# Fewer sparse products in the first two periods, six at the head of the later ones, and shorter scalar chains

## The chip, the core and the metric

One core of one Trainium2 chip runs the whole kernel in one launch. The metric is the device time of that launch in microseconds (us). Engines are named as in the profile: PE (TensorE matmul), PEld (its weight loads, which overlap PE), DVE (VectorE), ACT (ScalarE), POOL (GpSimd) and SP (SyncE, which issues most DMAs). Each engine runs its own instructions in program order and waits on semaphores for the others.

## The reference

```python
# x (2708, 256), adj (2708, 2708): about 0.3% of it nonzero, and its diagonal
x = layernorm(x + relu(concat([x, adj @ x], 1) @ weight + bias))      # layer 0

def top_p_attention(X):                 # W1, W3: (64, 256), W2: (64, 64)
    q = X @ W1.T @ W2.T
    k = X @ W3.T
    probs = softmax(q @ k.T)            # (2708, 2708)
    idx = argsort(-probs)
    sp = take_along_axis(probs, idx)
    cs = cumsum(sp)
    keep = cs - sp < 0.9                # the largest ones, up to 0.9 of the mass
    A = probs * scatter(keep, idx)
    return A / A.sum(-1)

R = adj + eye(N)
R = R / R.sum(-1)
Z, Xf, Xa = 0, x, x                     # layer 1
for n in range(2):
    A = top_p_attention(Xa)
    Xf = R @ Xf
    Xa = A @ Xa
    Z = Z + Xf @ U1[n].T + Xa @ U2[n].T
out = layernorm(x + layernorm(x + Z))   # the inner one with gain and bias
```

So there are two rounds of a 2708 x 2708 attention, in each of which every row is cut at 0.9 of its mass, and two products with a sparse matrix R.

## The kernel before

Rows are cut into 22 blocks of 128 (the last, the edge, has 20). The first part of the run, up to about 742 us, does layer 0, the first attention and the projections. The change lies in the second attention, a loop over 24 periods, `for per in range(NB + 2)`, each of six groups, `for g in range(NG)`. Some 23 to 26 us make a period, and in period `per` four blocks are in work at once:

- Block `per + 2` gets its logits and exponentials. The logits come in three chunks (L535 on PE, chunk 0 already in the last group of the period before, chunks 1 and 2 at groups 1 and 3). There is one buffer in PSUM for them, so a chunk waits until ACT has read the one before (L885, and L889 for a second, flatter exponential of chunk 0). L882 on DVE takes a row shift from chunk 0.
- Block `per + 1` is tried at two levels, on ACT (`try_act`): at each a pass with Relu (L1027) and one with Sign (L1030) over 2708 columns, and then a chain of operations on [128x1] numbers (L1033 to L1043) that gives the next level. DVE prepares the first level in `begin_search` (L893 to L898) and takes the results up in `last_level` (L1064 to L1074).
- Blocks `per` and `per - 1` are on DVE: one pass that drops what lies above the level (L1084), candidates (L1091), their order (L1100, L1103), a threshold (L1119 to L1139), marks (L1144), and the mask (L1149).
- Block `per - 2` is multiplied: PE turns the masked rows, four 128x128 tiles a group (`turn`, L562), ACT copies them from PSUM (L564), and PE multiplies them with `ya` (`products`, L591), two groups later.

Between these stand the products of R. Row block `m` of R is eight units, seven of gathered rows and one of its own rows, each one matmul of 256 columns (L788, two rows in the profile) summed in PSUM. There are two sweeps over the 22 row blocks, `s = 0` with `yf_d` and `s = 1` with `v_d`, the result of the first. With each unit POOL may issue one indirect DMA (`y_rows`, L745) that gathers rows for the unit two row blocks ahead; the gathered rows have three slots (`yg[:, m % 3]`). At the start of a row block SP issues the loads of R's part two row blocks ahead (`adjp` has three buffers). At its end DVE scales the sum and adds a base (`r_out`, L817 for the first sweep, `arrive`, L833 for the second), one or two groups later through the list `later`. Sixteen of the 352 units come before the loop; the number in a period is `units[per]`, and they are spread evenly over the six groups:

```python
n = n_r * (g + 1) // NG - n_r * g // NG
```

In group 0 they stand ahead of the block's first transposes, in later groups behind the transposes of the group. Periods 2 to 9 end the first sweep, period 10 has none, and periods 11 to 21 have the second sweep at 16 a period.

In the second sweep finished rows are normalised as they come (`final_slot`): statistics on DVE (L1240) at groups 3 and 4, L1276 and L1277 on ACT at group 5, and at group 0 of the next period L1250 on ACT and two adds and products on POOL (L1265, L1266), behind the gathers that POOL has been given up to then. What POOL leaves is what L1240 reads at group 4.

The small numbers of a block lie in one tile, `self.all`; `b.l0`, `b.l1`, `b.l2` are levels, `b.u0`, `b.u1` what lies above them, `b.few` and `b.kept` are used by `last_level`.

Of the kernel before, what the change touches and what calls it, by code (L numbers as in the profile page):

```python
# [11 lines left out]
AF = mybir.ActivationFunctionType  # L12
ALU = mybir.AluOpType
# [4 lines left out]
TOP_P = 0.9  # L18
# [15 lines left out]
STEPS = ((0.97048, 13.37709, 72.87486), (1.01755, 9.09506, 145.60103))  # L34
FEW = 17.8171
# [4 lines left out]
ML = 16  # L40
CW, CC = 128, 7
EARLY = 12
AT = 96


# [17 lines left out]
def gnn_two_layer_kernel(ctx: ExitStack, tc: tile.TileContext, N, xT_d, x_d, adj_d, w0_d, b0_d,  # L63
# [30 lines left out]
    assert SEG * (NS - 1) + 8 <= N <= SEG * NS == SEG2 * NS2 and N >= SEG2 * (NS2 - 1) + 8  # L94
    assert SEG * NS - P == (NB - 1) * P - AT and AT + N - (NB - 1) * P <= P
    assert NB == 3 * KS + 1 and CW == P and CAP % 8 == 0 and N < NB * P
# [63 lines left out]
def fast_path(ctx, tc, c, flags, fint, xT_d, x_d, w0_d, b0_d, w1_d, w2_d, w3_d, u1_d, u2_d, g_d, b_d):  # L160
    nc = tc.nc
    N, D, DA, NB, DC, KH, CHS, rows = c.N, c.D, c.DA, c.NB, c.DC, c.KH, c.CHS, c.rows
# [17 lines left out]
    def ps_acc(t=None):  # L180
        acc = ps.tile([P, CH], FP, tag="acc", name="acc")
        if t == NB - 1:
            nc.vector.memset(acc[:, :D + 1], 0.0)
        return acc
# [11 lines left out]
    b0 = es[1][:, :D]  # L196
# [272 lines left out]
    lists = Lists(0, ML, flags[:, NF - 4:NF - 2], first_room)  # L469
    order = list(range(EARLY)) + [EDGE] + list(range(EARLY, EDGE))  # L470
    for m, prev, then in zip(order, [None] + order, order[1:] + [None]):
# [37 lines left out]
        if ML <= m < EDGE:  # L509
            i, n = m - ML, EDGE - ML  # L510
# [14 lines left out]
    def logits(s, t, i):  # L525


        p = rows(t)
        lg = ps_lg()
        cs = KPS[2 * i:2 * i + 2]  # L530
        skip = CH - (cs[0][1] - cs[0][0])
        for h, (a, b) in enumerate(cs):
            o = slice(DA * h, DA * h + DA)
            at = (skip, 0)[h]
            nc.tensor.matmul(lg[:p, h, at:at + b - a], lhsT=q[o, t * P:t * P + p], rhs=keys[s][o, i, :b - a],  # L535
                             start=True, stop=True)
        a, b = cs[0][0], cs[-1][1]
        return lg.rearrange("p h n -> p (h n)")[:p, skip:skip + b - a], a, b
# [7 lines left out]
    NG = (NB + 3) // 4  # L546
# [80 lines left out]
    def exps1(t):  # L627

        p = rows(t)
        e = es[t % 4]  # L630
        nmax, srt = st1[t]
        z = small.tile([P, 2], FP, tag="z1", name="z1", bufs=3)
        st1[t] = (srt, z)
        h = 11 * P

        def part(i):
            if i == 0:
                nc.scalar.activation(srt[:p], srt[:p], AF.Exp, bias=nmax[:p], scale=1.0)
            a, b = ((0, h), (h, N))[i]
            nc.scalar.activation(e[:p, a:b], e[:p, a:b], AF.Exp, bias=nmax[:p], scale=1.0,  # L640
                                 accum_out=z[:p, i:i + 1])
        return part
# [46 lines left out]
    def ya_pair():  # L689
# [15 lines left out]
        p = rows(t0 + 1)  # L705
        nc.scalar.copy(ya[AT:AT + p, t0 + 1, :], pz[:p, 1, :])

# [95 lines left out]
    def za_load(m):  # L803


        if loads.get(m):
            loads[m] = 2
            return None
        loads[m] = 1
        base = work.tile([P, D], FP, tag="in", name="base", bufs=3)  # L810
        nc.sync.dma_start(out=base[:rows(m)], in_=za_d[m * P:m * P + rows(m), :])
        return base
# [36 lines left out]
    def e2(t):  # L849
        return ring[t % 5]  # L850
# [30 lines left out]
    def shift(b, lg):  # L881
        nc.vector.tensor_reduce(b.nmax, lg[:, :P], AX.X, ALU.max, negate=True)  # L882
# [8 lines left out]
    def begin_search(b):  # L891

        nc.vector.tensor_reduce(b.z, b.all[:b.p, :NL], AX.X, ALU.add)  # L893
        yield
        nc.vector.reciprocal(b.rz, b.z)
        nc.vector.tensor_scalar(b.nz, b.z, -1.0, None, op0=ALU.mult)
        yield
        nc.vector.tensor_scalar(b.l0, b.roots, b.roots, b.rz, op0=ALU.mult, op1=ALU.mult)  # L898

    def run_all(steps):  # L900
        for _ in steps:
            pass
# [22 lines left out]
    part = exps1(0)  # L925
# [5 lines left out]
    part = exps1(1)  # L931
# [11 lines left out]
    for t in range(NB):  # L943
        acc = ps_acc(t)
        part = exps1(t + 2) if t + 2 < NB else None
        b = None
        if t >= NB - 3:
            b = blocks[t - (NB - 3)] = Block(t - (NB - 3))
        ra_next = finish1(t + 1) if t + 1 < NB else None
        if t == 0:  # L950
            nc.vector.memset(x1_edge, 0.0)
            nc.vector.tensor_copy(x1_edge[AT:AT + rows(EDGE)], x1[:rows(EDGE), EDGE, :])
        for g in range(NG):
# [39 lines left out]
    scale, turn_out, project = ends  # L993
# [22 lines left out]
    def fifth():  # L1016
        nonlocal scr
        tile2 = big.tile([P, 2 * NW], FP, tag="V", name="e4")
        ring.append(tile2[:, :NW])
        scr = tile2[:, NW:]  # L1020

    def try_act(b, k, part):


        e = e2(b.t)[:b.p, :N]
        if part == 0:
            nc.scalar.activation(scr[:b.p, :N], e, AF.Relu, bias=b.nz, scale=b.l[k], accum_out=b.relu)  # L1027
            return
        if part == 1:
            nc.scalar.activation(scr[:b.p, :N], e, AF.Sign, bias=b.nz, scale=b.l[k], accum_out=b.sign)  # L1030
            return
        if part == 2:
            nc.scalar.activation(b.n, b.sign, AF.Identity, bias=halfn[:b.p], scale=0.5)  # L1033
            return
        nc.scalar.activation(b.u[k], b.relu, AF.Identity, bias=b.n, scale=b.rz)
        next_level(b, k)

    def next_level(b, k):
        keep, slope, down = STEPS[k]
        nc.scalar.activation(b.kept, b.l[k], AF.Copy, scale=keep + TOP_P * slope, bias=-down)  # L1040
        nc.scalar.activation((b.l1, b.l2)[k], b.u[k], AF.Identity, bias=b.kept, scale=-slope)
        if k:
            nc.scalar.activation(b.few, b.l1, AF.Copy, scale=TOP_P, bias=-FEW)  # L1043

    def level(b, l):

# [266 lines left out]

    each = NB * (CC + 1)
    first = 2 * (CC + 1)
    units = {0: 12, 1: 20}
    rest = each - first - sum(units.values())
    units.update({p: rest * (p - 1) // 8 - rest * (p - 2) // 8 for p in range(2, 10)})
    units.update({p: each * (p - 10) // 11 - each * (p - 11) // 11 for p in range(11, 22)})
# [3 lines left out]
    b0, b1, b2 = (blocks[t] for t in range(3))  # L1323
# [3 lines left out]
    try_dve(b0, 1)  # L1327
    run_all(begin_search(b2))
    try_act(b0, 1, 0)
    next_level(b0, 1)  # L1330
    lg = logits(1, 3, 0)
    r_units(CC + 1)
    r_outs()
# [2 lines left out]
    for per in range(NB + 2):  # L1336
        if per == 1:
            fifth()
        if per == NB + 1:
            tail.append(True)  # L1340
        n_r = units.get(per, 0)
        b_act = blocks.get(per + 1)
        t_mul = per - 2 if per > 1 else None
        if t_mul is not None:
            accs[t_mul] = ps_acc(t_mul)
        b_exp = None
        if per and per + 2 < NB:
            b_exp = blocks[per + 2] = Block(per + 2)
        vector = vector_slots(blocks.get(per), blocks.get(per - 1), begin_search(b_exp) if b_exp else None)
        for g in range(NG):  # L1350
            n = n_r * (g + 1) // NG - n_r * g // NG
            now = later.pop(0)
            later.append([])
            if g == 0:
                if b_exp:
                    shift(b_exp, lg[0])
                r_units(n)
            if t_mul == EDGE:
                if g == 0:
                    products(0)  # L1360
                    products(0)
                    edge_product(ya, accs[EDGE], e2(EDGE))
            elif t_mul is not None:
                turn(t_mul, g, ya, accs[t_mul], e2(t_mul))
            if b_exp and g == 3:
                lg = logits(1, b_exp.t, 2)
            if g == NG - 1 and 3 < per + 3 < NB:
                lg = logits(1, per + 3, 0)
            if g:
                r_units(n)  # L1370
            if b_exp and g == 1:
                lg = logits(1, b_exp.t, 1)
            if t_mul is not None and t_mul != EDGE:
                products(2)
            if b_exp and g in (0, 1, 3):
                exps2(b_exp, (g + 1) // 2, *lg)
            if b_act:
                for k, part in {0: ((0, 0),), 1: ((0, 1), (0, 2), (0, 3)), 2: ((1, 0),), 3: ((1, 1), (1, 2), (1, 3))}.get(g, ()):
                    try_act(b_act, k, part)
            if per == 0:  # L1380
                ya_pair()
            next(vector)
            if per == 2 and g == 1:
                nc.gpsimd.memset(ring[4][:, N:], 0.0)
            if g == 0:
                final_slot(0)
                if t_mul:
                    t = t_mul - 1
                    base = za_load(t)
                    later[1].append(lambda t=t, base=base: arrive(t, base, accs.pop(t), ras.pop(t)[:rows(t)]))  # L1390
            for f in now:
                f()
            if g and (per < NB + 1 or g < NG - 1):
                final_slot(g)
# [4 lines left out]
    for f in later[0] + later[1]:  # L1399
# [10 lines left out]
                                   op0=ALU.mult, op1=ALU.is_lt)  # L1410
# [9 lines left out]
    n = len(new) + len(finals)  # L1420
# [384 lines left out]
```

## Time and profile before

| what | value |
|---|---|
| median of 6 runs | 1307.95 us (1298.33 to 1315.97) |
| the profiled execution | 1303.53 us, its span 1301.7 us |
| PE busy over the span | 1206.0 us, 93% |
| DVE busy | 975.7 us, 75% |
| ACT busy | 733.4 us, 56% |
| POOL busy | 643.9 us, 49% |
| mean granted clock of TensorE | 0.972 |
| products of R (L788) after 742 us, each half a unit | 387 to 393 ns by the profile's rows |

The profile is of one execution. Matmuls overlap: a row of L788 is recorded as some 0.39 us, but in a run of them one starts about 0.22 us after another, so a unit of two rows takes 0.43 us of PE when PE runs on. The granted clock is given with stretches of the trace; at 0.50 a row takes twice as long. "issue" in brackets behind an idle time says that the profile shows nothing the engine waited for; for logits (L535) it is then the one buffer. Busy time over the whole span hides that the loop's stages have different bounds, so the tables that follow go by stretches of time.

### The profile page before, as it was taken

Reading aid. Unit: us, or ns where it says so; the run is one execution under the profiler, and the core shown is the slowest. Engines: PE = TensorE matmul, PEld = TensorE weight load, DVE = VectorE, ACT = ScalarE, POOL = GpSimd, SP = SyncE. Lnnn points to the kernel's source line nnn. Section 1 sums busy time; section 2 is a strip of 40 time slices with the busy share of each in tenths; the row PEclk is TensorE's granted clock in tenths of the full one; section 3 lists DMA queues with packets and bytes.
Section 4 is the critical chain, followed back from the end, with each engine's and each line's share of the span. In section 5 each row is a group of like instructions: output and inputs, shape, how many; then the busy total and the mean of one; then the engine's idle time right before and its main releaser. Section 6 shows DMA issues by size and latency. Waiting matters only on the chain.

```text
span 1301.7 us, 18668 instructions
## 1 busy us (share of the span) xinstructions
PE 1206.0 (93%) x5772; PEld 910.5 (70%) x5772; DVE 975.7 (75%) x3254; ACT 733.4 (56%) x1299; POOL 643.9 (49%) x596
## 2 busy tenths in 40 slices
PE   7999999999799999999996997999998899999875
PEld 6888878853577777766774575777776677776754
DVE  2455554976999888877751377898999889988886
ACT  2010111045565566655562478798999789988822
POOL 1000000014735533677566377788826868888860
PEclk9999999999899999999998798999999999999988
DMA  7465535434222110223223355565524545555441
GB/s 194 148 205 170 170 124 166 150 107 127 61 91 74 53 60 10 78 92 106 86 70 109 106 162 176 164 185 169 163 71 148 173 141 160 163 186 151 146 116 39
DMA packets 104248, 164.92 MB, mean 127 GB/s; under 512 B 20162, under 2 KB 76870, under 8 KB 104138
## 3 DMA queue, kind: packets, MB, share of 16 engines
q1 hardware_dynamic: 77852, 107.57, 25.9%
q0 software_dynamic: 20544, 51.17, 14.5%
q10 hardware_dynamic: 5742, 4.89, 1.4%
q8 instruction: 48, 0.79, 0.3%
q14 instruction: 62, 0.51, 0.1%
HBM read 129.66 MB, written 33.90 MB: 126 GB/s over the span
## 4 chain that ended last, share of the span: by engine, by line
PE 71%; ACT 10%; DVE 6%; issue 5%; POOL 3%; DMA 2%; another core or an unknown queue 2%; SPq 0%; ACTq 0%; POOLq 0%; DVEq 0%
PE acc L591 25%; PE acc L274 13%; PE lg L535 9%; PE misc L788 8%; PE tr L562 7%; POOL yg L745 3%; PE acc L678 2%; ACT e L885 2%; ACT e L1030 2%; PE acc L699 2%; ACT wT L564 2%; PE misc L727 1%; PE misc L449 1%; DMA yg<-v_d,ix 1%
## 5 line engine op out<-in xcount | busy, mean ns | idle before, releaser
L564 ACT COPY wT<-tr 128x512 f32<-128x512 f32 (+2 forms) x258 | 136.3, 537 | 232.9 <-PE tr L562 154.7
L591 PE MATMUL acc<-x,wT 128*128 128x256 f32 x882 | 222.6, 393 | 19.1 <-ACT wT L564 15.6
L745 POOL DMA_INDIRECT yg<-v_d,ix x154 | 197.1, 1280 | 76.6 <-issue 36.6
L591 PE MATMUL acc<-ya,wT 128*128 128x256 f32 x924 | 227.8, 388 | 3.6 <-issue 3.5
L745 POOL DMA_INDIRECT yg<-yf_d,ix x154 | 193.5, 1257 | 75.1 <-issue 36.1
L591 PEld LDWEIGHTS acc<-x,wT 128*128 128x128 f32 x882 | 161.4, 193 | 81.6 <-issue 31.5
L591 PEld LDWEIGHTS acc<-ya,wT 128*128 128x128 f32 x924 | 174.3, 193 | 43.9 <-issue 21.8
L274 PE MATMUL acc<-y,adj_t 128*128 128x257 f32 x924 | 204.4, 379 | 0.0
L274 PEld LDWEIGHTS acc<-y,adj_t 128*128 128x128 f32 x924 | 173.7, 189 | 26.8 <-issue 1.9
L384 POOL DMA_INDIRECT adj_t<-in_adj,ix x154 | 163.9, 1064 | 51.2 <-issue 43.7
L562 PE MATMUL tr<-ident,e 128*128 128x128 f32 (+1 forms) x946 | 147.7, 275 | 17.7 <-DVE e L1149 12.5
L535 PE MATMUL lg<-k,q 64*128 64x512 f32 (+3 forms) x528 | 139.8, 605 | 24.8 <-ACT e L542 9.4
L788 PE MATMUL misc<-yg,adj_t 128*128 128x256 f32 (+1 forms) x602 | 159.5, 393 | 2.1 <-DMA yg<-v_d,ix 1.9
L562 PEld LDWEIGHTS tr<-ident,e 128*128 128x128 f32 (+1 forms) x946 | 119.5, 144 | 54.6 <-issue 24.3
L351 POOL DMA_DIRECT2D part_d<-e x1 | 0.6, 576 | 274.1 <-DVE e L350 274.1
L788 PEld LDWEIGHTS misc<-yg,adj_t 128*128 128x128 f32 (+1 forms) x602 | 105.9, 190 | 41.5 <-issue 21.7
L1027 ACT ACTIVATE e<-e,st 128x2708 f32<-128x2708 f32 (+1 forms) x43 | 113.6, 2641 | 0.0
L1030 ACT ACTIVATE e<-e,st 128x2708 f32<-128x2708 f32 (+1 forms) x42 | 110.9, 2641 | 0.0
L462 ACT COPY x1T<-tr 128x256 f32<-128x256 f32 (+1 forms) x22 | 8.0, 364 | 174.6 <-PE tr L461 174.6
L597 DVE MAX8 cand<-e 128x8 f32<-128x170 f32 (+1 forms) x352 | 86.6, 319 | 21.3 <-ACT e L542 15.1
L1091 DVE MAX8 cand<-w 128x8 f32<-128x170 f32 (+1 forms) x352 | 94.4, 323 | 0.1
L535 PEld LDWEIGHTS lg<-k,q 64*128 64x128 f32 (+1 forms) x528 | 40.0, 185 | 57.7 <-issue 31.7
(254 smaller groups left out, 1799.8 us busy)
## 6 DMA issues: line engine op xcount, KB each, us to landing
adj_t<-in_adj SPq DMA_DIRECT2D x42, 704.0 KB
adj_t<-adjc_d SPq DMA_DIRECT2D x44, 448.0 KB
adjc_d<-adj_t SPq DMA_DIRECT2D x22, 256.0 KB
base<-za_d SPq DMA_DIRECT2D x40, 128.0 KB
adjc_d<-adj_t SPq DMA_DIRECT2D x22, 192.0 KB
xt<-in_x ACTq DMA_DIRECT2D x21, 128.0 KB
x_d<-x SPq DMA_DIRECT2D x21, 128.0 KB
x1b_d<-xb SPq DMA_DIRECT2D x21, 128.0 KB
```

The costliest lines, as they stand in the source:

```text
L274: nc.tensor.matmul(acc[:p, :n], lhsT=halves[k // KH][:, k % KH, :p], rhs=y[:, k, :n], start=k == 0, stop=stop and k == NB - 1)
L384: nc.gpsimd.indirect_dma_start(out=a[:CW, i, :], out_offset=None, in_=adj_rows, in_offset=bass.IndirectOffsetOnAxis(ap=ix[:CW, m, i:i + 1] ...
L535: nc.tensor.matmul(lg[:p, h, at:at + b - a], lhsT=q[o, t * P:t * P + p], rhs=keys[s][o, i, :b - a], start=True, stop=True)
L562: nc.tensor.transpose(tr[:, k % 4, :p], columns(e[:p], k), ident[:p, :p])
L564: nc.scalar.copy(wT[:, :len(ks), :p], tr[:, :len(ks), :p])
L591: nc.tensor.matmul(acc[:p, :D], lhsT=wT[:, k % 4, :p], rhs=part_y(y, k), start=k == 0, stop=k == NB - 1)
L597: nc.vector.max(dst[:p, i * 8:(i + 1) * 8], src[:p, i * step:i * step + w])
L745: nc.gpsimd.indirect_dma_start(out=yg[:CW, m % 3, i, :], out_offset=None, in_=rows_d, in_offset=bass.IndirectOffsetOnAxis(ap=ix[:CW, m, i: ...
L788: nc.tensor.matmul(acc[:p, :D], lhsT=a[:kw, k, :p], rhs=y[:kw, k, :] if k < CC else own[:p], start=k == 0, stop=k == CC)
L1027: nc.scalar.activation(scr[:b.p, :N], e, AF.Relu, bias=b.nz, scale=b.l[k], accum_out=b.relu)
L1030: nc.scalar.activation(scr[:b.p, :N], e, AF.Sign, bias=b.nz, scale=b.l[k], accum_out=b.sign)
L1091: nc.vector.max(b.cand[:p, 8 * i:8 * i + 8], low[:p, SEG2 * i:SEG2 * (i + 1)])
```

## The change

- `units` is 8 and 12 in periods 0 and 1 instead of 12 and 20. What is left over, 140 instead of 128, is spread over periods 2 to 9: 17 or 18 instead of 16.
- From period 2 on, six of a period's units (`HEAD`) stand in group 0, ahead of the first transposes, and the rest is spread over groups 1 to 5. With 16 units the groups have 6, 2, 2, 2, 2, 2 instead of 2, 3, 3, 2, 3, 3. Each unit takes its gather, its loads and its `r_out` along.
- The small chain of the first level on ACT no longer passes through `b.u0`: `begin_search` prepares a scale and an offset on DVE (two more [128x1] operations a block), and the chain writes `b.l1` in its second operation. `b.kept` and `b.few`, which hang on `b.l1` alone, follow it there (`from_level`) instead of in the second level's chain. The first chain keeps four operations, the second has three instead of five.

```diff
--- before.py
+++ after.py
@@ -40,6 +40,7 @@
 ML = 16
 CW, CC = 128, 7
 EARLY = 12
+HEAD = 6
 AT = 96
 
 
@@ -895,7 +896,10 @@
         nc.vector.reciprocal(b.rz, b.z)
         nc.vector.tensor_scalar(b.nz, b.z, -1.0, None, op0=ALU.mult)
         yield
+        keep, slope, down = STEPS[0]
         nc.vector.tensor_scalar(b.l0, b.roots, b.roots, b.rz, op0=ALU.mult, op1=ALU.mult)
+        nc.vector.tensor_scalar(b.m, b.rz, -slope, None, op0=ALU.mult)
+        nc.vector.tensor_scalar(b.d, b.l0, keep + TOP_P * slope, -down - slope * N / 2, op0=ALU.mult, op1=ALU.add)
 
     def run_all(steps):
         for _ in steps:
@@ -1029,18 +1033,23 @@
         if part == 1:
             nc.scalar.activation(scr[:b.p, :N], e, AF.Sign, bias=b.nz, scale=b.l[k], accum_out=b.sign)
             return
+        if part == 2 and k == 0:
+            nc.scalar.activation(b.n, b.sign, AF.Identity, bias=b.d, scale=-STEPS[0][1] / 2)
+            return
         if part == 2:
             nc.scalar.activation(b.n, b.sign, AF.Identity, bias=halfn[:b.p], scale=0.5)
             return
-        nc.scalar.activation(b.u[k], b.relu, AF.Identity, bias=b.n, scale=b.rz)
-        next_level(b, k)
-
-    def next_level(b, k):
-        keep, slope, down = STEPS[k]
-        nc.scalar.activation(b.kept, b.l[k], AF.Copy, scale=keep + TOP_P * slope, bias=-down)
-        nc.scalar.activation((b.l1, b.l2)[k], b.u[k], AF.Identity, bias=b.kept, scale=-slope)
-        if k:
-            nc.scalar.activation(b.few, b.l1, AF.Copy, scale=TOP_P, bias=-FEW)
+        if k == 0:
+            nc.scalar.activation(b.l1, b.relu, AF.Identity, bias=b.n, scale=b.m)
+            from_level(b)
+            return
+        nc.scalar.activation(b.u1, b.relu, AF.Identity, bias=b.n, scale=b.rz)
+        nc.scalar.activation(b.l2, b.u1, AF.Identity, bias=b.kept, scale=-STEPS[1][1])
+
+    def from_level(b):
+        keep, slope, down = STEPS[1]
+        nc.scalar.activation(b.kept, b.l1, AF.Copy, scale=keep + TOP_P * slope, bias=-down)
+        nc.scalar.activation(b.few, b.l1, AF.Copy, scale=TOP_P, bias=-FEW)
 
     def level(b, l):
 
@@ -1313,7 +1322,7 @@
 
     each = NB * (CC + 1)
     first = 2 * (CC + 1)
-    units = {0: 12, 1: 20}
+    units = {0: 8, 1: 12}
     rest = each - first - sum(units.values())
     units.update({p: rest * (p - 1) // 8 - rest * (p - 2) // 8 for p in range(2, 10)})
     units.update({p: each * (p - 10) // 11 - each * (p - 11) // 11 for p in range(11, 22)})
@@ -1327,7 +1336,8 @@
     try_dve(b0, 1)
     run_all(begin_search(b2))
     try_act(b0, 1, 0)
-    next_level(b0, 1)
+    from_level(b0)
+    nc.scalar.activation(b0.l2, b0.u1, AF.Identity, bias=b0.kept, scale=-STEPS[1][1])
     lg = logits(1, 3, 0)
     r_units(CC + 1)
     r_outs()
@@ -1349,6 +1359,9 @@
         vector = vector_slots(blocks.get(per), blocks.get(per - 1), begin_search(b_exp) if b_exp else None)
         for g in range(NG):
             n = n_r * (g + 1) // NG - n_r * g // NG
+            if per > 1 and n_r:
+                ahead = min(n_r, HEAD)
+                n = (n_r - ahead) * g // (NG - 1) - (n_r - ahead) * (g - 1) // (NG - 1) if g else ahead
             now = later.pop(0)
             later.append([])
             if g == 0:
```

## The prediction

> **What bounds the kernel now.** I read the chain that ended last first, for what the end of the run hangs on; then the table by stage; then, where a stage has gaps, the timeline and the list of waits.
>
> ```profile
> PE 71%; ACT 10%; DVE 6%; issue 5%; POOL 3%; DMA 2%; another core or an unknown queue 2%; SPq 0%; ACTq 0%; POOLq 0%; DVEq 0%
> ```
>
> PE is 71% of the chain over the whole span, but the change touches only the loop over periods, from about 742 us on, and there the bound changes from stage to stage. The next table has PE, PEld, DVE, ACT and POOL busy time, the granted clock and DMA for stretches that I chose.
>
> ```profile
> 753.30:769.40 16.10, 14.35 (x66) 12.06 (x65) 11.06 (x48) 15.79 (x23) 11.27 (x11) 1.00 0.60 190
> 772.60:790.20 17.60, 13.42 (x50) 8.93 (x50) 13.19 (x37) 17.30 (x26) 14.51 (x11) 0.89 0.60 186
> 787.40:790.80 3.40, 3.40 (x10) 2.77 (x9) 1.10 (x7) 2.66 (x7) 2.49 (x4) 0.50 0.51 142
> 797.60:804.40 6.80, 6.04 (x16) 3.88 (x17) 6.49 (x29) 6.80 (x8) 5.23 (x7) 0.50 0.40 118
> 834.30:969.70 135.40, 133.73 (x658) 103.00 (x657) 121.47 (x414) 119.72 (x191) 96.07 (x70) 1.00 0.52 151
> 1067.00:1138.70 71.70, 69.81 (x341) 53.13 (x340) 69.86 (x235) 68.83 (x117) 60.04 (x51) 1.00 0.54 161
> 1164.30:1241.10 76.80, 66.54 (x320) 51.90 (x318) 66.56 (x234) 63.52 (x109) 63.95 (x55) 0.98 0.52 158
> ```
>
> Periods 0 and 1 (first two rows) belong to ACT: 15.79 busy of 16.10 us, 17.30 of 17.60. Periods 3 to 9 belong to PE: 133.73 of 135.40. Periods 12 to 15 are shared by PE (69.81 of 71.70) and ACT (68.83). Periods 17 to 20 belong to none of PE, DVE and ACT; the waits below say why. Now PE between periods 1 and 2, and ACT's one row there; columns are start, duration, engine and line, and in brackets the idle time before.
>
> ```profile
> 786.32 1.13 PE L535 MATMUL lg<-k,q 64*128 64x512 f32 x4 [3.74 <-issue]
> 787.38 2.93 PE L788 MATMUL misc<-yg,adj_t 128*128 128x256 f32 x6
> 790.10 0.94 PE L788 MATMUL misc<-adj_t 128*128 128x256 f32 x2
> 790.87 1.03 PE L788 MATMUL misc<-yg,adj_t 128*128 128x256 f32 x4
> 791.74 1.04 PE L562 MATMUL tr<-ident,e 128*128 128x128 f32 x8
> ...
> 798.36 2.08 PE L535 MATMUL lg<-k,q 64*128 64x512 f32 x4 [4.29 <-issue]
> ```
> ```profile
> 795.20 0.59 ACT L564 COPY wT<-tr 128x512 f32<-128x512 f32 x1 [5.04 <-PE misc L788]
> ```
>
> PE waits 3.74 us for the single logits buffer, which ACT frees at 786.2; six products of R (12 rows) follow at half clock, then the first transposes. ACT, idle 5.04 us, takes them at 795.20. Last, the waits from 1013 us on.
>
> ```profile
> PE tr L562 <- DVE e L1149: 12.5, 4, 5.1
> ```
> ```profile
> DVE bst L1240 <- POOL u L1266: 9.5, 9, 2.2
> ```
> ```profile
> POOL u L1265 <- ACT u L1250: 17.8, 2, 9.7
> ```
>
> From period 16 PE waits for the mask, DVE (ahead of the mask) waits for POOL's L1266, and POOL waited only twice for the data of its L1265: in between it is a standing queue. One period of POOL there is 14 gathers at 1.25 us from start to start, two of them 2.6 us longer (rows of 3.5 us), and four adds at 0.8: 17.5 + 5.2 + 3.2 = 25.9 us, against 25.7 from mask to mask.
>
> **The change, part by part.**
>
> *Twelve products of R leave periods 0 and 1 for periods 2 to 9.* One unit is two rows of L788 on PE, 0.43 us (790.10 at half clock: 0.77). It brings one gather on POOL for seven units in eight, and per eight units three loads and a store on SP's queue and one DVE row L817 of 0.48.
>
> In periods 0 and 1 the 12 units free 5.2 us of PE, but ACT sets the pace there and does no more and no less. L817, for which DVE waits 4.23 us at 762.64, moves behind the threshold, so the mask of 772.67 comes about 4.4 us sooner; DVE then meets ACT again at 786.30 (L893 after the last exponential), where it waits 1.79 us now and would wait about 6. I count nothing; the bounds are 0 and -4.4.
>
> In periods 2 to 9 the 12 units land on a full PE: 12 x 0.43 = +5.2 us (about 0.65 a period). Bounds: +5.2, and -1.7 less than that, the PE idle time in 834.3 to 969.7. The gathers moved ask 2.19 row blocks x 11.1 us = 24.3 us of POOL a period of 23.5, a deficit of 0.8 x 8 = 6.4 us; POOL is done early (3.77 us busy in 947.9 to 969.7), so some 18 us cover it. Without that cover the 6.4 us would show. SP's loads stay two row blocks ahead, as now; with six units in front they are issued at most one group (4 us) sooner, past the loads and stores of the last norm. PE waited for no such load in the whole loop (its only DMA waits are 1.9 us for gathers): 0.
>
> The Trainium skill, Perfetto Trace Analysis, Identifying the Most-Contended Engine, says that matmul busy time is a poor measure of how full TensorE is and that weight-load busy time is better. In the row above that is 103.00 of 135.40, 76%; by it PE would have room and the 5.2 would be near 0. I go by the row's gaps (1.7 us in 135) and by starts that follow each other without a break.
>
> *Six units ahead of the first transposes.* Between the logits' first chunk (last group of the period before) and the first transposes there were 6 units in period 2 and 5 later (884 to 887, 906 to 909). Now there are 8 in period 2, 9 in periods 3 to 9 and 8 from 12 on. All of that lies in series: ACT frees the logits, PE does logits, units, transposes, ACT copies. Period 2: 2 units more, 0.86 at full clock, 1.7 at half: I take +1.3, for the stretch is at half clock until 790.8. Periods 3 to 9: from the transposes (end 887.77) to the next period's logits (904.62) are 16.85, of which ACT waited 1.16 in the middle; from there to the transposes' end (910.27) 5.65, and now 4 x 0.43 more: 16.85 - 1.16 + 5.65 + 1.72 = 23.1, under PE's 23.5. Hidden, with 0.4 us to spare; if ACT's 1.16 remains, 24.2, +0.7 a period, +5 in all. Periods 12 to 15: ACT runs without a gap from 1096.36 to 1113.80, 17.44, then 5.5 + 1.29: 24.2 instead of 23.2, +1.0 x 4 = +4.0. But POOL's queue is late next: from period 16 it sets 25.7 whatever PE did before, so the 4.0 are taken out of DVE's waits for L1266 (9.5 us). I count 0; without that cover +4.0.
>
> On POOL four more gathers stand ahead of the first L1265 (48 for v_d instead of 44), 4 x 1.25 = 5.0, at most 7.6 with a slow one. They fall into the 8.09 us that POOL idles before 1057.19, so L1265 and L1266 keep their times and the four gathers are gone from the end (8 left behind the last instead of 12). The tail gains what PE waits for gathers in the last periods, 1.9 us (0.37, 0.91, 0.64 at 1228.8, 1256.5, 1261.1): I take -1.5, bounds 0 and -5.0. PE's waits for the mask, 2 to 5 us each, are filled with R, but the mask's own time is POOL's: 0.
>
> *Shorter chains on ACT.* At 781.57 the first chain takes 1.17 us; its four operations stay four, without the step of 0.39 us from one number to the next: 1.04 by the starts of the same rows. The second, 1.23 at 788.93, has three instead of five: 0.95. So -0.4 us a block on ACT, of which the path sees periods 0 and 1: -0.5 in all (two first chains, and the second one of period 0, ahead of the copies at 768.37). Elsewhere PE or POOL covers it. DVE gets two [128x1] rows a block, 0.13 (L896) to 0.27 (L898) each, 0.4 a block; it has 13.9 us idle in 135.4: nothing, but 0.4 a period (+8) if DVE were the bound. DVE's L1064 no longer waits 2.20 at 790.19 for the chain's last operation; the next thing late is the level two rows on, 0.3 earlier: nothing.
>
> *The clock.* After idle times of 1.75, 3.74 and 4.29 us the granted clock was 0.50 for 3.4, 3.4 and 6.8 us. With fewer units in periods 0 and 1 PE idles longer there. Bounds: 0, and one more stretch of 3.4 us at half clock, +1.7. I take 0 beyond the 1.3 above, since ACT's end, not PE's, decides how long.
>
> The Trainium skill, TensorE: Matmul & The Clock Gate, Part 1 (The HAM clock gate), states that about 3.4 us of idling halves the clock and about 3.4 us of work restores it. The 3.74 and 4.29 agree; the 1.75 doesn't, and the trace decides. The rule speaks against taking work out of periods 0 and 1: by it a longer wait could cost the 1.7 again, and the sum would be 6.2.
>
> *Sum:* -0.5 + 1.3 + 5.2 + 0 - 1.5 = +4.5. The profiled execution took 1303.53 us, so 1308.0; the median of the runs is 1307.95, 4.4 above it, and the forecast in its terms is 1312. Runs of this kernel lie 1298 to 1316, so about 1% is what can be told from no change.
>
> **The rivals.**
>
> *Forecast, 0.50:* 1312, its own range 1305 to 1319.
>
> *PE had room, 0.13:* the units that move cost nothing in periods 2 to 9. For it: PEld at 76%, POOL and ACT not full. Against: rows without gaps. -0.7: 1307.
>
> *Periods 0 to 2 shrink, 0.15:* the products of R are what holds DVE (4.23), and through PE the half clock (10.2 us at half, 5.1 lost) and ACT's 5.04. If all three go, 14.4 us are won; the 5.2 stay, and the tail gives its whole bound: 1308 - 14.4 + 5.2 - 5.0 = 1294. It decides if the copy at 795.20 comes within 2 us of ACT's last step. For it: DVE is 28.88 busy in the 33.6 us from 772.7. Against: ACT's full rows, and 8 units instead of 6 before the transposes at 792.
>
> *POOL's adds come later, 0.22 (slower):* the four gathers do not fit into the idle time before the first L1265, because they are released only when PE has done the six units. L1265, L1266, DVE's L1240, the mask and the transposes then move by 5.0 us, and nothing absorbs the 4.0 of periods 12 to 15; the tail's 1.5 are not won. 1312 + 5.0 + 4.0 + 1.5 = 1322.5. It decides as soon as the fourth gather ends later than L1250 delivers: by 7.6 of 8.09 us the margin is 0.5.
>
> **How the numbers follow.** Slower by over 1% (past 1321) is the last rival, with a small part of it below the line and some of the forecast's edge above: 0.23. Faster by over 1% (under 1295) is most of the third: 0.14. Within 1%: 0.63. The range, 1297 to 1327, leaves out the best of the third case and a POOL rival with the clock's 1.7 and DVE's share on top.
>
> **What would show it.** Right: masks of periods 3 to 9 spaced 0.6 wider, their stretch still PE-bound; the first transposes of period 2 about 1 us later against the period's start; POOL's idle time before its first L1265 down from 8.1 to 0.5 to 3; PE's 12.5 us for the mask smaller, but masks from 16 on still 25.7 apart; PE's waits for gathers gone. Wrong: masks of 3 to 9 no wider apart, ACT idle less than 5 us before period 2's first copy, half clock gone from 787 to 804, or the masks from 16 on closer or later by 5.

## The result and the profile after

The changed kernel takes 1318.19 us (median of 20 runs, 1305.24 to 1330.1), the kernel before, with more runs, 1306.17. The ratio is 1.0087, 95% interval 1.0065 to 1.0110: about 11.4 us slower. The forecast was 1312, 4.5 us slower; the rival in which POOL's adds come later gave 1322.5. The profiled execution took 1324.17 us, span 1321.8, which is 6.0 above the median; the one of the kernel before (1303.53) is 2.6 below its own, so the two profiles lie further apart than the medians. Lines of code have moved: L788 is L789, L562 is L563, L564 is L565, L885 and L889 are L886 and L890, L1149 is L1158, L1240 is L1249, L1265 is L1274.

The table by stage, in the changed kernel's own stretches (periods 0 and 1, the half clock, periods 3 to 9, 13 to 15, 17 to 19):

```profile
757.00:773.00 16.00, 13.36 (x60) 10.81 (x59) 12.47 (x50) 15.26 (x21) 11.16 (x10) 1.00 0.50 135
775.60:792.80 17.20, 9.75 (x34) 5.28 (x33) 12.92 (x39) 16.96 (x25) 13.08 (x10) 0.83 0.40 119
786.90:793.70 6.80, 4.52 (x10) 2.57 (x11) 2.91 (x18) 5.83 (x9) 4.29 (x5) 0.50 0.57 172
833.80:980.30 146.50, 139.91 (x680) 107.13 (x679) 124.47 (x429) 118.83 (x181) 94.74 (x77) 1.00 0.54 157
1086.70:1159.30 72.60, 67.91 (x328) 51.39 (x328) 70.20 (x241) 65.24 (x108) 60.66 (x52) 1.00 0.56 169
1184.00:1260.10 76.10, 70.16 (x345) 55.01 (x344) 67.35 (x241) 67.18 (x110) 63.53 (x54) 1.00 0.51 155
```

ACT still fills periods 0 and 1 (16.96 of 17.20); PE has less to do there (9.75 instead of 13.42). Periods 3 to 9, from mask to mask, take 146.5 us instead of 135.4, with PE 139.91 busy instead of 133.73 and idle for 6.6 us instead of 1.7. The pass between periods 1 and 2, on PE and then ACT:

```profile
789.18 2.08 PE L536 MATMUL lg<-k,q 64*128 64x512 f32 x4 [4.37 <-ACT e L1031]
791.19 3.69 PE L789 MATMUL misc<-yg,adj_t 128*128 128x256 f32 x10
794.71 0.59 PE L789 MATMUL misc<-adj_t 128*128 128x256 f32 x2
795.14 1.03 PE L789 MATMUL misc<-yg,adj_t 128*128 128x256 f32 x4
796.00 1.04 PE L563 MATMUL tr<-ident,e 128*128 128x128 f32 x8
```
```profile
796.64 0.59 ACT L565 COPY wT<-tr 128x512 f32<-128x512 f32 x1 [3.81 <-PE tr L563]
```

Eight units (16 rows) stand between the logits and the first transposes. ACT starts to copy those at 796.64, while the profile's row of the transposes still runs (to 797.04); in the kernel before, 2.4 us lay between the end of the transposes (792.78) and the copy at 795.20. The waits from 990 us on:

```profile
PE tr L563 <- DVE e L1158: 6.6, 2, 4.7
```
```profile
DVE bst L1249 <- POOL u L1275: 2.6, 3, 0.9
```
```profile
POOL u L1274 <- ACT u L1259: 24.6, 2, 14.4
```

PE waits less for the mask and DVE less for POOL, and POOL waits longer for L1259, of which 10.26 us lie before its first add. The first add before (first line) and after:

```profile
1057.19 0.73 POOL L1265 TENSOR_TENSOR u<-u,gb 128x256 f32<-128x256 f32 x1 [8.09 <-ACT u L1250]
```
```profile
1076.86 0.73 POOL L1274 TENSOR_TENSOR u<-u,gb 128x256 f32<-128x256 f32 x1 [10.26 <-ACT u L1259]
```

Shorter waits of PE and DVE look like a gain; yet the first add comes at 1076.9 instead of 1057.2. Ahead of it lies a stretch (1031 to 1046 us), called the slow stretch below, in which PE starts one instruction in 0.7 to 2.1 us for no reason that the profile shows:

```profile
1037.32 0.38 PE L592 MATMUL acc<-ya,wT 128*128 128x256 f32 x1 [0.50 <-issue]
1038.06 0.46 PE L592 MATMUL acc<-ya,wT 128*128 128x256 f32 x1 [0.37 <-issue]
...
1040.15 1.01 PE L592 MATMUL acc<-ya,wT 128*128 128x256 f32 x2 [1.63 <-issue]
```

The kernel before has such a stretch too, shorter, from 1036 to 1046 us:

```profile
1038.23 0.38 PE L591 MATMUL acc<-ya,wT 128*128 128x256 f32 x1 [1.72 <-issue]
1040.34 3.05 PE L591 MATMUL acc<-ya,wT 128*128 128x256 f32 x5 [1.74 <-issue]
```

### The profile page after: what moved, and what is told of

It is laid out like the page before. It is cut to its first block, busy times and chain, and to the rows that moved or that the text cites. A ratio compares the mean times of both kernels' runs of the same rounds, so it can differ in the third digit from the quotient of the medians.

```text
span 1321.8 us, 18660 instructions
## 1 busy us (share of the span) xinstructions
PE 1212.7 (92%) x5772; PEld 910.1 (69%) x5772; DVE 983.0 (74%) x3298; ACT 727.9 (55%) x1257; POOL 634.1 (48%) x596
## 4 chain that ended last, share of the span: by engine, by line
PE 67%; ACT 14%; DVE 9%; issue 5%; DMA 2%; POOL 1%; another core or an unknown queue 1%; SPq 0%; ACTq 0%; POOLq 0%; DVEq 0%
PE acc L592 23%; PE acc L275 12%; PE lg L536 9%; PE misc L789 8%; PE tr L563 6%; ACT e L886 3%; PE acc L679 2%; ACT e L1034 2%; ACT wT L565 2%; ACT e L1031 2%; PE misc L450 1%; PE misc L728 1%; ACT e L890 1%; PE acc L491 1%; DMA xT<-in_xT 1%
## 5 line engine op out<-in xcount | busy, mean ns | idle before, releaser
L565 ACT COPY wT<-tr 128x512 f32<-128x512 f32 (+2 forms) x258 | 136.5, 537 | 255.0 <-PE tr L563 177.2
L746 POOL DMA_INDIRECT yg<-yf_d,ix x154 | 183.4, 1191 | 87.6 <-issue 35.2
L385 POOL DMA_INDIRECT adj_t<-in_adj,ix x154 | 171.9, 1117 | 51.7 <-issue 43.5
L563 PE MATMUL tr<-ident,e 128*128 128x128 f32 (+1 forms) x946 | 149.8, 278 | 14.4 <-DVE e L1158 6.6
L789 PE MATMUL misc<-yg,adj_t 128*128 128x256 f32 (+1 forms) x602 | 158.3, 391 | 2.2 <-DVE h L834 1.3
L563 PEld LDWEIGHTS tr<-ident,e 128*128 128x128 f32 (+1 forms) x946 | 119.4, 144 | 53.8 <-issue 22.5
L789 PEld LDWEIGHTS misc<-yg,adj_t 128*128 128x128 f32 (+1 forms) x602 | 105.9, 189 | 39.2 <-issue 22.5
```

The source lines that it names most:

```text
L385: nc.gpsimd.indirect_dma_start(out=a[:CW, i, :], out_offset=None, in_=adj_rows, in_offset=bass.IndirectOffsetOnAxis(ap=ix[:CW, m, i:i + 1] ...
L563: nc.tensor.transpose(tr[:, k % 4, :p], columns(e[:p], k), ident[:p, :p])
L565: nc.scalar.copy(wT[:, :len(ks), :p], tr[:, :len(ks), :p])
L746: nc.gpsimd.indirect_dma_start(out=yg[:CW, m % 3, i, :], out_offset=None, in_=rows_d, in_offset=bass.IndirectOffsetOnAxis(ap=ix[:CW, m, i: ...
L789: nc.tensor.matmul(acc[:p, :D], lhsT=a[:kw, k, :p], rhs=y[:kw, k, :] if k < CC else own[:p], start=k == 0, stop=k == CC)
```

## The experiments

Twelve kernels ran in three groups of four, each beside the kernel before on the same chip. The first group ran on a chip on which the kernel before takes 1303.64 us, much as in the result above (whose chip is not on record); the other two on one on which it takes 1256 us. Times by stage, in us, are taken from the profiles: from the first product of `ya` (L699) to the first ACT copy of the second multiplied block (periods 0 to 2), from there to that of the tenth (to period 10), to that of the sixteenth (to period 16), and to the end. "Apart" below means from the first ACT copy of one multiplied block to that of the next. Each row of stages is one execution: the profiled one of the kernel before on the second chip (1259.38 us) is 3.4 us above the median of its runs, so differences of 2 or 3 us between two rows are not firm, and the ratio of the runs decides.

First chip (the first two rows are the profiles shown so far and the ratio above):

| kernel | ratio (95%) | 0-2 | 3-10 | 11-16 | to the end | sum |
|---|---|---|---|---|---|---|
| before | 1 | 82.1 | 178.6 | 144.4 | 158.9 | 563.9 |
| changed | 1.0087 (1.0065-1.0110) | 79.0 | 189.1 | 157.8 | 154.5 | 580.4 |
| units alone | 1.0015 (0.9988-1.0041) | 75.5 | 184.9 | 144.4 | 161.8 | 566.7 |
| head alone | 1.0088 (1.0059-1.0117) | 87.9 | 182.2 | 158.5 | 149.1 | 577.6 |
| chains alone | 1.0027 (1.0000-1.0055) | 82.8 | 181.0 | 142.0 | 161.4 | 567.2 |
| head, 2nd sweep | 1.0030 (1.0000-1.0061) | 83.3 | 180.2 | 154.0 | 150.4 | 567.9 |

Second chip:

| kernel | ratio (95%) | 0-2 | 3-10 | 11-16 | to the end | sum |
|---|---|---|---|---|---|---|
| before | 1.0006 (0.9996-1.0017) | 76.2 | 176.3 | 136.4 | 161.4 | 550.3 |
| changed | 1.0126 (1.0109-1.0144) | 77.7 | 182.0 | 144.4 | 160.6 | 564.8 |
| units alone | 1.0048 (1.0031-1.0064) | 76.2 | 180.8 | 136.4 | 160.5 | 554.0 |
| units and chains | 1.0069 (1.0053-1.0086) | 75.8 | 180.6 | 140.2 | 159.9 | 556.5 |
| head, 1st sweep | 1.0036 (1.0022-1.0050) | 79.9 | 176.6 | 138.6 | 159.2 | 554.3 |
| head, three behind | 1.0087 (1.0069-1.0106) | 79.3 | 177.5 | 145.8 | 158.9 | 561.5 |
| period 10 | 1.0077 (1.0062-1.0092) | 75.2 | 182.0 | 143.4 | 159.7 | 560.3 |
| more units | 0.9993 (0.9982-1.0005) | 76.5 | 172.7 | 138.5 | 159.3 | 547.1 |

**The parts one by one (first chip).** Units alone:

```diff
-    units = {0: 12, 1: 20}
+    units = {0: 8, 1: 12}
```

> The kernel before with one part of the change alone: 8 and 12 units in periods 0 and 1, the 12 units more in periods 2 to 9; no units at the head, the old chains. Theory A (the units land on a full PE): 12 x 0.43 = +5 us, ratio 1.004, masks of periods 3 to 9 about 0.65 us wider apart, and 0 to -3 us in periods 0 to 2. Theory B (the six units at the head are the whole cost, through the serial stretch between the first logits and the first transposes): 0 to -3 us, ratio 0.998 to 1.000. Theory C (the 12 us are only a longer slow stretch around period 11 that falls differently in each build): no change before period 10.

+6.3 us in periods 3 to 10 and -6.6 in 0 to 2, in this profile: A's cost is there, and a gain that I had not counted (A allowed up to -3). Theories B and C both fail on periods 3 to 10.

Head alone, in the kernel before:

```diff
+HEAD = 6
...
             n = n_r * (g + 1) // NG - n_r * g // NG
+            if per > 1 and n_r:
+                ahead = min(n_r, HEAD)
+                n = (n_r - ahead) * g // (NG - 1) - (n_r - ahead) * (g - 1) // (NG - 1) if g else ahead
```

> The kernel before with six units ahead of the first transposes from period 2 on; 12 and 20 units, old chains. Theory A: periods 2 to 9 hidden under PE (0 to +1 us), periods 12 to 16 wider by 1.1 us each and given back from 17 on (25.7 becomes about 24.4): 0 to +3 us, ratio 1.000 to 1.002. Theory B: ACT idles 3 to 4 us instead of 1.1 at each period's first copy and PE no longer runs through: +8 to +12 us, ratio 1.006 to 1.009, of which half in periods 2 to 9. Theory C: as before outside period 11.

12.4 us slower (1316.04 against 1303.64), as much as the whole change; B by the total, A by what happens in periods 14 to 16 (24.5 apart instead of 23.2) and 17 to 20 (22 to 24.5 instead of 25.7). Ahead of period 11, 9.4 us are lost (5.8 and 3.6), where A had 0 to 1 and B half of its 8 to 12: that speaks for B. And 8.6 us of the difference between the profiles is in one period, the 12th, with the slow stretch, which neither theory has.

Chains alone (the changed kernel with 12 and 20 units and the old spread):

> The kernel before with the shorter chains on ACT alone, and their two operations a block more on DVE; 12 and 20 units, old spread. Theories A and B: -0.5 us by the chain in periods 0 and 1, up to -2 if ACT's steps (0.23 shorter at the first level by the changed kernel's rows) count in periods 12 to 16 too: ratio 0.998 to 1.000. Rival D (DVE is the bound from period 16 on and its 0.4 us a block shows): +2 to +4 us, ratio 1.002 to 1.003.

Between 0 and 7 us slower, no gain. Its blocks from 17 on are 25.8 to 26.0 apart, before 25.5 to 25.9, so D's 0.4 a block isn't shown in this profile.

Head from period 11 on, `per > 10` in place of `per > 1`:

> The kernel before with six units ahead of the first transposes only from period 11 on (the second sweep); everything else as before. Theory A: +1.1 us in each of periods 12 to 16, given back from 17 on, and the end up to 1.5 us sooner: -1.5 to +1 us, ratio 0.999 to 1.001. Theory B: +4 to +6 us that stay, ratio 1.003 to 1.005. The rival of the prediction (POOL's L1265 five us later): masks from 16 on 5 us later, +5 us or more.

0 to 8 us slower by the runs. POOL idles 9.01 us before its first add even with 48 gathers ahead of it, so the first add isn't held up by gathers here: the cover that the prediction counted on is there, on this chip. The period with the slow stretch takes 33.5 us, though, against 29.4.

**The second chip.** The next four kernels ran on a chip without these stretches. Head in periods 2 to 9 only, `1 < per < 10`:

> The kernel before with six units ahead of the first transposes only in periods 2 to 9 (the first sweep); everything else as before. Theory B1 (the head costs in periods 1 to 9, since PE waits there for ACT: +6 up to period 2's second copy, +2 to +3 in periods 3 to 9): +8 us, ratio 1.006, and the second half as before, its slow stretch around period 11 or 12 too (29 us from copy to copy). Rival E (the head costs in the second sweep, through the slow stretch, which was 4 to 7 us longer in the three kernels that have it there): 0 to +2 us, ratio 1.000 to 1.002.

+4.5 to 5 us by the ratio, of which 3.7 lie in periods 0 to 2 (there 20 units in period 1 put ten, not eight, ahead of the first transposes) and 0.3 in 3 to 10. So B1 has the place right and the size of periods 3 to 10 wrong: they are 22.5 apart, 0.2 more than before.

A third unit kept in the group behind the first transposes:

```diff
+HEAD = 6
...
+            if per > 1 and n_r:
+                rest_r = n_r - HEAD - 3
+                n = (HEAD, 3)[g] if g < 2 else rest_r * (g - 1) // 4 - rest_r * (g - 2) // 4
```

> As the run with the head alone (12 and 20 units, old chains), but the group behind the first transposes keeps three units, as before the change, instead of two: 6, 3, 1, 2, 2, 2 of 16. Theory N (the head takes a unit from the stretch in which ACT does the two exponentials of the first chunk, so PE reaches the second chunk too early and waits 0.2 to 1.1 us for L890 in every period): that wait falls under 0.3, periods 3 to 9 come back to 22.5 to 23, and the ratio to the kernel before falls from 1.0088 to about 1.006; what is left is period 1 and 2 and the second sweep. Rival: the wait is only pushed to another place, ratio 1.008 to 1.010.

Theory N falls for the first sweep: periods 3 to 9 are 22.5 apart with three units behind and with two. The rival holds: from 783 to 944 us PE waits for L890 only once (7 times in the changed kernel on this chip), but six times for L886, 1.0 us in all. The ratio is no better than with the head alone, though that ran on the other chip. The cost here is 9.4 us in periods 11 to 16, with POOL's first add at 1019.1 instead of 1011.4.

The changed kernel without its head:

> The changed kernel without the six units at the head: 8 and 12 units and the short chains, old spread. If the head is the whole cost and the parts add up: ratio 1.000 to 1.004 (units alone 1.0015, chains alone 1.0027), the loop's first three periods about 7 us shorter than before and periods 3 to 9 about 5 longer. If the units and the head only cost together (PE too full for the serial stretch): ratio 0.998 to 1.001. If chains and units cost whatever the head does: 1.006 or more.

Units and chains alone cost 0.69%: above the first bracket, in the third (they cost whatever the head does). In periods 0 to 2 nothing is won on this chip (75.8 against 76.2), in 3 to 10 4.3 are lost, as forecast; 3.8 us are lost in periods 11 to 16, where these two parts move nothing but the chains.

The left-over units in period 10:

```diff
-    units = {0: 12, 1: 20}
+    units = {0: 8, 1: 12, 10: 12}
...
+            if per == 10:
+                n = n_r // 3 if g < 3 else 0
```

> The kernel before with 8 and 12 units in periods 0 and 1, 16 in periods 2 to 9 as before, and the 12 left over in period 10, which had none, in its first three groups; old spread and old chains. By the profiles, 8 and 12 units make periods 0 to 2 about 7 us shorter, and the 5 us that they cost in periods 3 to 9 fall away; period 10 has some 3 us of PE idle time for 5 us of units: -5 us, ratio 0.996. Rival: the second sweep's first gathers start some 10 us later, POOL's queue is the bound of the second half, and the end comes up to 10 us later: ratio 1.003 or more.

The rival holds, and the expected gain is not there: period 10 takes 25.2 us instead of 20.6, so periods 3 to 10 are 5.7 us longer, and 7.0 more are lost in periods 11 to 16, with POOL's first add at 1019.9 instead of 1011.4.

**The same chip, four kernels together.** The kernel before and the changed one themselves:

> The kernel before itself, for a profile on the same chip as the runs beside it. The last four kernels ran on a chip where the kernel before takes 1256 us, not 1304, and where the stretches are missing in which PE starts one instruction in 0.7 to 2.1 us (near 700 and near 1036 us). On such a chip: ratio 1.000, periods 3 to 9 spaced 22.3, periods 12 to 16 as 23.2, period 17 on 25.7, start of the loop to period 2's second copy 63 to 68 us. If the slow stretches are a matter of the profile and not of the chip, they are back at 700 and 1036.

> The changed kernel itself, beside the kernel before on the same chip. If the parts add up (units and chains 1.0069 without the head, head in the first sweep 1.0036, a second sweep about 1.003): 1.011 to 1.014. If the slow stretches were behind most of the 1.0087, as theory C has it, and this chip has none: 1.003 to 1.006. If they cost together what the dearest costs alone: 1.007 to 1.009.

The kernel before has no slow stretch on this chip, periods 3 to 9 are 22.3 apart and 17 on 25.7. The changed one is 1.26% slower, 15.8 us, which is in the bracket in which the parts add up; on this chip no slow stretch is needed to make the change slow. The deciding lines are POOL's, its first gather of `v_d` and the rows around its first add. Before:

```profile
944.40 0.94 POOL L745 DMA_INDIRECT yg<-v_d,ix  x1 [30.41 <-DMA v_d<-base]
...
1009.14 0.94 POOL L745 DMA_INDIRECT yg<-v_d,ix  x1 [0.30 <-PE lg L535]
1010.39 0.95 POOL L745 DMA_INDIRECT yg<-v_d,ix  x1 [0.30 <-PE tr L562]
1011.36 0.76 POOL L1265 TENSOR_TENSOR u<-u,gb 128x256 f32<-128x256 f32 x1
```

After:

```profile
948.93 0.94 POOL L746 DMA_INDIRECT yg<-v_d,ix  x1 [32.25 <-DMA v_d<-base]
...
1020.75 0.95 POOL L746 DMA_INDIRECT yg<-v_d,ix  x1 [0.30 <-PE misc L789]
1022.00 0.95 POOL L746 DMA_INDIRECT yg<-v_d,ix  x1 [0.30 <-issue]
1022.97 0.74 POOL L1274 TENSOR_TENSOR u<-u,gb 128x256 f32<-128x256 f32 x1
```

There is no idle time before the first add in either. It comes 67.0 us after POOL's first gather of `v_d` before (944.4), and 74.0 after (948.9): four gathers more at 1.25, and 2.1 for longer gathers. The 48 gathers follow each other with 0.3 us between, so PE does not hold them up. From then on the first adds of successive periods are 24.8 to 25.7 apart before and 25.5 to 25.8 after (the last two steps aside), so the delay stays to the end. All eight profiles of this chip say the same: from the first product of `ya` to POOL's first add they differ by 15.3 us (302.1 to 317.4), from there to the end by only 2.4 (245.0 to 247.4), so the loop is as late as POOL's first add. DVE and PE show it. Before:

```profile
DVE bst L1240 <- POOL u L1266: 13.6, 11, 2.2
```
```profile
PE tr L562 <- DVE e L1149: 12.1, 4, 4.5
```

After, where the blocks are 25.7 apart from period 15 on instead of 17:

```profile
DVE bst L1249 <- POOL u L1275: 23.1, 16, 2.2
```
```profile
PE tr L563 <- DVE e L1158: 14.5, 7, 4.6
```

In periods 3 to 9 PE is the whole bound on this chip, before (first line) and after:

```profile
783.50:939.20 155.70, 155.70 (x767) 119.57 (x766) 143.20 (x487) 139.26 (x224) 105.51 (x83) 1.00 0.51 154
```
```profile
783.30:943.70 160.40, 159.22 (x781) 122.24 (x781) 141.55 (x499) 137.28 (x210) 107.18 (x87) 1.00 0.53 159
```

> The units alone again (8 and 12, old spread, old chains), to part them from the chains in the ratio 1.0069 of both. Theory A (12 x 0.43 us on a full PE, nothing won in periods 0 to 2, where ACT sets the pace): +5 us, ratio 1.004, periods 3 to 9 at 22.9 from copy to copy. If the profiles of the first chip hold (periods 0 to 2 shorter by 7 us): -2 to 0 us, ratio 0.998 to 1.000, and the 1.0069 is the chains'.

+6.0 us by the runs, periods 3 to 9 alternately 22.7 and 23.1 apart (17 and 18 units), nothing won in periods 0 to 2: theory A.

> The other way round: the kernel before with 16 and 28 units in periods 0 and 1, and 14 or 15 instead of 16 in periods 2 to 9. If ACT sets the pace of periods 0 and 1 whatever PE has to do there, and PE that of 3 to 9: -12 x 0.43 = -5 us less what ACT's own loop stops at (21.6 us a period against 22.3): -4 us, ratio 0.997, the best of all. If products of R in periods 0 and 1 do hold PE's logits and transposes up, as on the first chip: 0 to +3 us, ratio 1.000 to 1.002.

16 and 28 units in periods 0 and 1: 3.6 us won in periods 3 to 10 and 0.3 lost in 0 to 2, as the first bracket has it. In periods 11 to 16 2.1 go again and come back to the end, so this profile's loop is 3.2 us shorter; the runs show 0.9993 (0.9982 to 1.0005), no difference. No version here beats the kernel before.

## Why the prediction was right, and where it was not

The range (1297 to 1327) holds 1318.19, and so does the forecast's own, 1305 to 1319, by 0.8 us. That is in part luck: the sum was +4.5 and the runs show +11.4, nearer to the 14.6 of the rival in which POOL's adds come later. The direction and the term of the units came out; two terms of the head did not.

- **Units.** +5.2 was right: 4.5 us in periods 3 to 10 on the second chip and 1.0048 by the runs. The Trainium skill (Perfetto Trace Analysis, Identifying the Most-Contended Engine) has the headroom of TensorE judged by MFU and weight-load time instead of matmul busy time; by the 76% of weight-load time the term would have been near 0. The runs decide against that here: the rows without gaps told more than the 76%. "I count nothing" for periods 0 and 1 holds on the second chip (76.2 with 20 units and with 12). On the first, one profile shows 6.6 us won there.
- **Head, period 2.** +1.3 expected; 77.7 against 75.8 without the head on the second chip, +1.9.
- **Head, periods 3 to 9.** "Hidden, with 0.4 us to spare" is nearly right: 182.0 against 180.6, +1.4 of the 5 that the upper bound allowed. PE waits for L890 there (7 times, 1.2 us in all), since the stretch behind the transposes lost a unit; a third unit put back only moved the waits to L886. On the first chip it is not hidden: 189.1 against 184.9 with the units alone, and the head alone 182.2 against 178.6, most of the +5 that the prediction named as the price if ACT's wait remains. In the changed kernel's row of 146.50 us PE is idle for 6.6, of which 4.0 before logits that wait for L886 and L890, and 2.3 with nothing shown.
- **Head, periods 12 to 15.** The 24.2 a period were measured as 24.4 and 24.5 on the first chip, and given back from 17 on, as said.
- **Head on POOL: the step that failed.** The prediction let four gathers fall into "the 8.09 us that POOL idles before 1057.19". That idle time is found where the slow stretch is: 8.1 to 11.3 us in the six profiles that have it, at most 0.5 in the eight of the chip without it. There the term is not 0 and -1.5 but +5.0: 305.1 us from period 10's end on with the head (144.4 + 160.6), 300.1 without (140.2 + 159.9). The first add comes 74.0 us behind the first gather instead of 69.9. It is the price of four gathers and the mechanism of the rival that I gave 0.22; its reason (gathers released late by PE) is not what happened. On the first chip the idle time stays (10.26 us), so the gathers did fit, and some of the tail's gain is there (from POOL's first add to the end 239.8 to 244.9 us with a head in the second sweep, 244.5 to 247.7 without). But there the slow stretch itself is longer in all three kernels with such a head (the period with it 33.5 to 38.0 us, against 27.6 to 29.4 in the three without). The prediction had no term for it, and why it is longer stays open.
- **Chains.** -0.5 expected: -0.4 in periods 0 to 2 on the second chip. After period 10 the profile with units and chains loses 3.2 us beside the units alone, and POOL's first add comes 69.9 us after its first gather instead of 67.0 with the same 44 gathers. The 22 long gathers take 77.4 us there and 72.1 with the units alone. Why, no run tells; and since the two ran in different groups and their intervals overlap (1.0069 and 1.0048), the loss itself is not sure.
- **Clock.** Around the wait of 4.37 us the clock was 0.50 for 6.8 us (3.4 with 3.74 before), but the stretch of half clock behind it is 3.4 instead of 6.8, and the 3.4 near 770 us are gone. From 740 to 830 us the mean granted clock is 0.94 instead of 0.92, so the bound of 1.7 was not reached, and the 0 holds.
- **The sum.** By the second chip's profiles: 4.5 (units) + 1.9 + 1.4 + 5.0 (head) + 2.6 (chains: -0.4, -0.2, +3.2) - 0.9 (the units' own end) = 14.5, which is 564.8 - 550.3. The forecast's 4.5 had the units and period 2; it lacked POOL's 5.0, 1.4 of the head on PE, and the chains' 3 if they are real. On the first chip the two profiles differ by 16.5 us in the loop (-3.1, +10.5, +13.4 and -4.4 by stage), 7.3 of them in the period with the slow stretch (36.7 against 29.4); the runs have 11.4, and no run splits these.

Open: what the slow stretches are, why a head makes the one near 1036 us longer, and the long gathers. A kernel with the head's products but with its gathers left in their old groups was not run; it would part POOL's share from PE's.

## What to carry to other kernels

Idle time in one profile is cover only if you know what made it: here it stood beside a disturbance that another chip does not have, and on that chip the work meant for it cost its full price, four gathers at 1.25 us, in a queue that nothing behind could outrun. Work taken from an engine that does not set the pace won nothing on that chip (76.2 us in periods 0 to 2, with and without it), and put on one that does it cost about what its rows take. When a later stage is paced by a queue of its own (POOL's here), ask of every gain before it whether that queue starts sooner; if not, the gain is gone by the end.

## What the runs showed of the hardware

The same program took 1303.64 us on one chip and 1256 us on another. The spans of the two profiles differ by 44.1 us: 30.4 of them lie before the loop, 5.9 in periods 0 to 2 (82.1 against 76.2), and 7.1 in the period with the slow stretch (29.4 against 22.3). In that stretch, in the changed kernel's profile, PE starts instructions 0.7, 1.4 or 2.1 us apart while POOL goes on at 1.25 us a gather. In each of the six profiles with times near 1310 PE has 13 to 36 idle times before which the profile shows nothing that it waited for ("issue"), in the eight with times near 1260 not one, whatever the kernel; so, as far as these profiles show, they go with the chip. The profile doesn't name their cause.
